# Layer 0 of a two-layer graph attention kernel: a pair's two aggregations in one set of matmuls, the tiles' chains staggered anew, and another order of loads and block sums at the begin

## Chip, core and metric

The kernel runs on one core of a Trainium2 chip. The metric is the device time of one execution in microseconds. One launch computes both layers, in float32 throughout.

## What is computed

The input `x` has 128 graphs of 64 nodes with 768 features, `adj` is a boolean adjacency per graph. Layer 0 is an additive graph attention with a gate, layer 1 a dot-product attention with six heads. Each is followed by a residual and a layer normalization. Cut to what matters here, layer 0 is:

```python
h = einsum('bnd,ade->bane', x, W)                 # 12 heads of 64
th = tanh(h)
attn = th @ w_src + swapaxes(th @ w_dst, 2, 3)    # rows + columns
attn = where(attn >= 0, attn, 0.2 * attn)
attn = softmax(where(~adj, -999.0, attn), axis=-1)
f = elu(einsum('banm,bame->bane', attn, h) + b)   # the aggregation
gate = sigmoid(x @ H_w.T + H_b)
x = layernorm(x + gate * f + (1 - gate) * x)
```

Layer 1 forms queries, keys and values with `Wq`, `Wk`, `Wv`, takes a masked softmax per head, and projects with `Wf`.

## The kernel before

Two graphs make a tile of 128 rows (nodes) by 768 features, so there are 64 tiles. Two tiles make a pair (`p` from 0 to 31, its tiles `i` = 0 and 1). Layer 0 (`phase_a`) goes over the pairs, and layer 1 (`phase_b`) over groups of two pairs.

**Dense products.** A product of a pair's two tiles with a 768 by 768 matrix is done with seven block products in place of eight, over sums of token blocks (`sums`, on POOL, L263 to L266) and sums of weight blocks (`weight_sums`, L178). Each of the seven is a *dense step* (`dense`): three matmuls of 128 by 128 by 384, two records each in the trace (L214), and an eviction. The evictions of i = 0, 2 and 3 are copies on ACT into `snap` (L439); those of i = 1, 4 and 5 are additions on DVE (L462, for V L481); that of i = 6 is a copy on ACT (L460, for V L479). The accumulators X (i = 0, 2, 4, 6), Z (i = 1) and Y (i = 3, 5) live in four PSUM banks (`psX`). Since i = 2 adds into the bank that i = 0 filled, its matmuls wait until the snap of i = 0 is taken; likewise i = 4 for the snap of i = 2, i = 5 for that of i = 3, and i = 6 for the addition of i = 4. Layer 0 does three products per pair: W gives h, G the gate's input, and V (a few pairs later, from the finished x1) layer 1's values.

**A tile's chain** (`Tile0`). From h: `tanh` (ACT, L499); products with `w_dst` and `w_src` (POOL, L503 and L511); their sums (DVE, L506 and L515) and a transpose (L508); the destination row goes out to DRAM and comes back over all partitions (`dst_out`, `dst_in`, L521 and L529, on SP's queue); `exchange` swaps halves of h by DMA (`hx`, L539); `add` (twelve ACT instructions, L553); `mask` and `top` (DVE, L560 and L564); `exp` (twelve ACT instructions, L569); `scale` (DVE reciprocal L577, POOL L579); `probs` (six transposes on TensorE, L590, and two copies on ACT, L595); `aggregate` (24 matmuls of 64 by 64 by 64, L608); `elu` (DVE L629, ACT L636); `mix1` and `mix2` (DVE, L641, L642, L650, L651); `norm1` (DVE L305 to L316 and three small ones on POOL, L317 to L322); `norm2` (ACT, L326); `spill` (DMA). `gate_in` (POOL, L618) and `gate` (ACT, L622) prepare the gate. x is loaded twice: as rows (`load`, into `xb`), and in blocks (`xp`), which DVE transposes (L418) into T.

**The order** is written out by hand: `at(step, f)` puts f into a list for its step, and `run` emits the lists in order of steps. Within a step the functions come in the order in which they were put there, pair by pair; the older pair's come first. Each engine works through its instructions in exactly this order. Pair p begins at step `O[p]`; below, o is that step:

```python
O = [14 * p if p < 3 else 21 * p - 21 for p in range(NP)]
...
for i, s in ((1, o), (0, o + (4 if p == NP - 1 else 5))):
    ...
    at(s + 24, t.probs)
    at(s + 25, t.aggregate)
    at(s + 26, t.elu)
```

In the steady state (21 steps a pair) W has steps 0 to 6 of a pair's slot, G 7 to 13, and V of the pair three before it 14 to 20; the chain of the slot's pair runs on into the next slot. Tile 1's chain starts with s = o, tile 0's with s = o + 5. So tile 1 is aggregated at step 25 (step 4 of the next slot) and tile 0 at step 30 (step 9). A few buffers are shared: one `th`, one `tmp`, one `z`, one `pt` (also the result of `elu`'s exponential), two `xp`, and four PSUM banks `pa`, of which an aggregation takes two until its `elu` has read them.

**The begin.** The first pair's x, the adjacency and W's four blocks are loaded in this order on SP's queue. The first pair's T comes from TensorE transposes (L433). DVE forms four weight block sums for each of three c before the first sum-dependent step, for W and later for H (`w1`), whose rows TensorE transposes (`hw_blocks`, L390).

Of the kernel before, what the change touches and what calls it, by code (L numbers as in the profile page):

```python
# [9 lines left out]
F32 = mybir.dt.float32  # L10
# [5 lines left out]
P = 128  # L16
# [45 lines left out]
def kernel(  # L62
# [31 lines left out]
    nc = tc.nc  # L94
    NB, S, D = x.shape
# [7 lines left out]
    NP = NT // 2  # L103
    assert S == 64 and DH == P and E == 64 and HALF == 384 and A == 12

    x_t = x.rearrange("(t g) n d -> t (g n) d", g=2)
# [7 lines left out]
    xb = const.tile([P, 7, D], F32, name="xb")  # L114
# [29 lines left out]
    def weight_tile(tag):  # L144
        return wts.tile([P, 7, CH, HALF], F32, name=f"w{tag}", tag=f"w{tag}")
# [28 lines left out]
    def weight_sums(part, eng, ks=range(4)):  # L174

        for k in ks:
            to, a, b = ((3, 6, 4), (4, 4, 0), (2, 6, 4), (5, 1, 2))[k]
            eng.tensor_tensor(part(to), part(a), part(b), ALU.subtract)  # L178
# [11 lines left out]
    def act_blocks(Ta, Tb, Ss):  # L190

        return [
            lambda c: Ta(c),
            lambda c: Ta(CH + c),
            lambda c: Ss(1, c),
            lambda c: Ss(2, c),
            lambda c: Ss(0, c),
            lambda c: Tb(CH + c),
            lambda c: Ss(3, c),
        ]  # L200
# [128 lines left out]
    def phase_a(ctx):  # L329
        k6 = ctx.enter_context(tc.tile_pool(name="k6", bufs=2))  # L330
        k3 = ctx.enter_context(tc.tile_pool(name="k3", bufs=1))
# [4 lines left out]
        st = [dict() for _ in range(NP)]  # L336
# [12 lines left out]
        def load_adj(p):  # L349
            t = small.tile([P, 2, S], U8, name="adj")  # L350
            nc.sync.dma_start(t, adj_p[p])
            st[p]["adj"] = t

        def load(p):
            st[p]["x"] = []
            for i in range(2):
                t = xb[:, (0, 1, 5, 6)[(2 * p + i) % 4]]
                nc.sync.dma_start(t, x_t[2 * p + i])
                st[p]["x"].append(t)

        load(0)
        load_adj(0)

        w0 = weight_tile(0)
        w0_v = w0.rearrange("p s c o -> p s (c o)").rearrange(
# [3 lines left out]
        for kh, oh in ((0, 0), (1, 0), (0, 1), (1, 1)):  # L369
            nc.sync.dma_start(  # L370
                w0_v[:, SLOT[kh, oh]],
                W_v[kh][:, oh * 6 : (oh + 1) * 6],
            )
        w1 = weight_tile(1)
        hrows = {}

# [65 lines left out]
        def sums(d):  # L442
            Ss = k6.tile([P, 4, CH, P], F32, name="S")
            token_sums(Ss, *d["T"])
            d["S"] = Ss

        def product(d, rhs, sink):
            Ta, Tb = d["T"]
            Ss = d["S"]
            blocks = act_blocks(lambda c: Ta[:, c, :], lambda c: Tb[:, c, :], lambda k, c: Ss[:, k, c, :])  # L450
            return Product(
                lambda i, c: blocks[i](c), rhs, [P, HALF], snap, sink
            )
# [36 lines left out]
        class Tile0:  # L490
            def __init__(self, p, i):
                self.p, self.i, self.d = p, i, st[p]
                self.sd = sds[i]
                self.last = p == NP - 1

            def tanh(self):
                self.h = self.d["h"][self.i]
# [84 lines left out]

            def probs(self):

                self.pt = k3.tile([P, D], F32, name="pt").rearrange("p (j n) -> p j n", n=P)
                for q in range(2):
                    ps = psa.tile([P, CH, P], F32, name="pa")
                    for jj in range(CH):
                        j = q * CH + jj
                        nc.tensor.transpose(  # L590
                            ps[:, jj, :],
                            self.s[:, 2 * j : 2 * j + 2, :].rearrange("p h m -> p (h m)"),
                            ident,
                        )
                    nc.scalar.copy(self.pt[:, q * CH : (q + 1) * CH, :], ps)  # L595
# [76 lines left out]
        def at(step, *fs):  # L672
            events.setdefault(max(step, 0), []).extend(fs)
# [6 lines left out]
            d[key].evict(i)  # L680

        for c in range(CH):
            at(0, lambda c=c: weight_sums(lambda s: w0_v[:, s, :, c, :], nc.vector))
            for k in range(4):
                at(
                    13 + 4 * c + k,
                    lambda c=c, k=k: weight_sums(lambda s: w2[:, s, c], nc.gpsimd, [k]),
                )
# [11 lines left out]
        for p in range(NP):  # L700
            d, o = st[p], O[p]
            d["p"] = p
            if p:
                at(max(o - 20, 1), lambda p=p: load_adj(p))
                at(o + 10, lambda p=p: load(p))

            def xb_in(d, i):
                d.setdefault("xp", []).append(blocks(x_t[2 * d["p"] + i]))

            def xT(d, i):  # L710
                d.setdefault("T", []).append(turn(d["xp"][i]))

            if p:
                at(max(o - 20, 1), lambda d=d: xb_in(d, 0))
                at(max(o - 16, 1), lambda d=d: xb_in(d, 1))
                at(o - 6, lambda d=d: xT(d, 0))
                at(o - 5, lambda d=d: xT(d, 1))
                at(o - 4, lambda d=d: sums(d))
            else:
                at(0, lambda d=d: d.update(T=[transposed(t) for t in d["x"]]))  # L720
                at(0, lambda d=d: sums(d))
            at(o, lambda d=d: start_h(d))
            at(o + 7, lambda d=d: start_g(d))
            for i in range(7):
                at(o + i, lambda d=d, i=i: dense(d, "W", i))
                at(o + 7 + i, lambda d=d, i=i: dense(d, "G", i))
            for i, s in ((1, o), (0, o + (4 if p == NP - 1 else 5))):
                t = Tile0(p, i)
                at(s + 6 + (i == 0), t.tanh, t.cap)
                at(s + 7, t.dst_mul)  # L730
                at(s + 8, t.src_mul)
                at(s + 9, t.dst_sum, t.dst_out)
                at(s + 10, t.src_sum)
                at(s + 13, t.dst_in)
                at(s + 16, t.exchange)

                at(s + (15 if i else 17), lambda t=t: t.add(0))
                at(s + (16 if i else 17), lambda t=t: t.add(1))
                at(o + (14 if i else 16), t.gate_in)
                at(o + (17 if i else 18), t.gate)  # L740
                n = s - (i == 1)
                at(n + 18, t.mask, t.top)
                at(n + 19, lambda t=t: t.exp(0))
                at(n + 20, lambda t=t: t.exp(1))
                (at_front if i else at)(s + 21, lambda t=t: t.scale(0), lambda t=t: t.scale(1))
                at(s + 24, t.probs)
                at(s + 25, t.aggregate)
                at(s + 26, t.elu)
                at(s + 27, t.mix1)
                at(s + 28, t.mix2)  # L750
                at(s + 29, t.norm1)

                n = s + (0 if p == NP - 1 else 1)
                at(n + 30, t.norm2)
                at(n + 31, t.spill)

            def x1_in(d, i):
                d["xp", i] = blocks(x1_d[2 * d["p"] + i])

            def x1T(d, i, t):  # L760
                d["x1T", i] = t
                nc.sync.dma_start(xT_d[d["p"]][:, i], t)

            def x1_sums(d):
                d["T"] = [d["x1T", i] for i in range(2)]
                sums(d)

            if p < NP - 3:
                v = O[p + 3] + 14
                times = ((1, v - 19, v - 13), (0, v - 16, v - 10))  # L770
            elif p < NP - 1:

                v = O[-1] + (21 if p == NP - 3 else 28)
                times = ((1, v - 16, v - 7), (0, v - 15, v - 6)) if p == NP - 3 else (
                    (1, v - 13, v - 6), (0, v - 10, v - 5)
                )
            if p < NP - 1:
                for i, t0, t1 in times:
                    at(t0, lambda d=d, i=i: x1_in(d, i))
                    at(t1, lambda d=d, i=i: x1T(d, i, turn(d["xp", i])))  # L780
                at(times[1][2] + 1, lambda d=d: x1_sums(d))
            else:
                v = o + 45
                for i in range(2):
                    at(o + 43 - i, lambda d=d, i=i: x1T(d, i, transposed(d["x"][i])))
                at(o + 44, lambda d=d: x1_sums(d))
            at(v, lambda d=d: start_v(d))
            for i in range(7):
                at(v + i, lambda d=d, i=i: dense(d, "V", i))

        for c in range(CH):
            at(4 + c, lambda c=c: weight_sums(lambda s: w1[:, s, c], nc.vector))


        early_sums = {"S": {}}
# [1 line left out]
        o = O[-1]  # L797
# [477 lines left out]
```

## Time and profile before

| | |
|---|---|
| median of three runs | 2848.83 us (2848.54 to 2848.85) |
| profiled execution, its own time | 2848.75 us |
| its span, first to last instruction | 2847.0 us |
| mean granted TensorE clock | 0.997 |
| layer 0 (to the first L904 matmul) | about 1466 us |
| layer 1 | about 1381 us |
| TensorE idle, from the span and its busy time | 40.4 us |

The profiled execution stands for the runs: it differs from their median by 0.1 us. The page gives each engine's busy share, the span in 40 slices, and the chain of work that ended last. A row of a timeline is: start in us from the span's start, duration, engine, line, operation, output<-inputs, shapes, count, and in brackets the engine's idle time just before and what ended it. A row of the chain of waits is: start, duration, and the work on the chain. PE is TensorE's matmuls, DVE VectorE, ACT ScalarE, POOL GpSimd, and SP the queue that issues all DMAs.

### The profile page before, as it was taken

How to read it: one execution, taken by the hardware profiler on the slowest of the kernel's cores; microseconds unless marked ns; L12 is line 12 of the kernel's file. 1: busy time of each engine (PE TensorE's matmuls, PEld its weight loads, DVE VectorE, ACT ScalarE, POOL GpSimd, SP SyncE). 2: the span in 40 equal slices, each digit the busy share in tenths (PEclk: the TensorE clock that was granted, in tenths of full speed). 3: DMA queues.
4: the chain of work that ended last, by engine and by line, in shares of the span. 5: the costliest groups of instructions: out<-in, count | busy, mean ns of one | idle time of the engine just before them, and what ended most of it. 6: DMA issues, size and time to landing. Idle time of an engine off the chain costs nothing.

```text
span 2847.0 us, 50750 instructions
## 1 busy us (share of the span) xinstructions
PE 2806.6 (99%) x18108; PEld 2062.2 (72%) x18108; DVE 1853.4 (65%) x3724; ACT 1198.5 (42%) x3737; POOL 1546.6 (54%) x1653
## 2 busy tenths in 40 slices
PE   8899999999999999999999999999999999999998
PEld 5555565655655665556568888888888888888887
DVE  4887777877877777777764555555555555555556
ACT  4666656566565665656622211222211222211223
POOL 4755556555566555565536555446554456454455
PEclk9999999999999999999999999999999999999999
DMA  6434445345454454444551211212211212211222
GB/s 170 121 113 139 142 132 146 114 138 147 127 146 126 132 149 123 143 133 133 181 180 35 90 67 63 85 57 90 90 65 60 90 57 90 89 62 63 90 84 73
DMA packets 358684, 308.40 MB, mean 108 GB/s; under 512 B 226592, under 2 KB 304160, under 8 KB 358432
## 3 DMA queue, kind: packets, MB, share of 16 engines
q1 hardware_dynamic: 358432, 305.16, 34.7%
q8 instruction: 144, 2.36, 0.3%
q14 instruction: 108, 0.88, 0.1%
HBM read 191.41 MB, written 101.06 MB: 103 GB/s over the span
## 4 chain that ended last, share of the span: by engine, by line
PE 87%; DVE 5%; POOL 3%; DMA 2%; ACT 2%; issue 1%; SPq 1%; DVEq 0%; ACTq 0%; POOLq 0%
PE X L904 43%; PE X L214 37%; PE pb L1051 2%; PE pb L969 2%; PE pa L608 1%; PE pa L590 1%; DMA s<-dst_d 1%; PE pb L1027 1%; ACT s L553 1%; DVE z L650 1%; ACT s L569 1%; DVE z L641 1%; DVE s L560 0%; DVE w L178 0%; POOL w L178 0%
## 5 line engine op out<-in xcount | busy, mean ns | idle before, releaser
L214 PE MATMUL X<-w,S 128*128 128x384 f32 x2304 | 795.0, 490 | 9.8 <-DVE w L178 3.3
L214 PEld LDWEIGHTS X<-w,S 128*128 128x128 f32 x2304 | 429.9, 190 | 297.6 <-DVE w L178 5.2
L904 PE MATMUL X<-S,w 128*128 128x256 f32 x2752 | 635.4, 379 | 0.0
L214 PE MATMUL X<-w,T 128*128 128x384 f32 x1728 | 600.7, 490 | 7.6 <-ACT snap L439 6.1
L904 PEld LDWEIGHTS X<-S,w 128*128 128x128 f32 x2752 | 518.1, 190 | 68.0
L214 PEld LDWEIGHTS X<-w,T 128*128 128x128 f32 x1728 | 325.9, 191 | 235.7 <-ACT snap L439 18.5
L947 DVE TENSOR_TENSOR xs<-xs,X 128x256 f32<-128x256 f32 x512 | 210.0, 419 | 175.0 <-PE X L904 166.5
L904 PE MATMUL X<-w,Sc 128*128 128x256 f32 x1280 | 294.4, 381 | 0.3 <-DVE xs L947 0.3
L569 ACT ACTIVATE s<-s,nmx 128x64 f32<-128x64 f32 x768 | 256.2, 335 | 76.5 <-DVE nmx L564 76.5
L930 DVE TENSOR_TENSOR k<-k,X 128x256 f32<-128x256 f32 x320 | 132.8, 418 | 231.9 <-PE X L904 160.2
L904 PEld LDWEIGHTS X<-w,Sc 128*128 128x128 f32 x1280 | 241.6, 190 | 34.3 <-DVE xs L947 1.1
L930 DVE TENSOR_TENSOR q<-q,X 128x256 f32<-128x256 f32 x320 | 133.1, 419 | 193.6 <-PE X L904 153.8
L904 PE MATMUL X<-xb,w 128*128 128x256 f32 x1024 | 258.0, 382 | 0.4 <-ACT q L925 0.4
L326 ACT ACTIVATE xs<-xs,shift,rstd 128x768 f32<-128x768 f32 x62 | 63.5, 1024 | 436.6 <-POOL shift L322 425.6
L439 ACT COPY snap<-X 128x384 f32<-128x384 f32 x288 | 135.5, 470 | 229.0 <-PE X L214 226.2
L925 ACT ACTIVATE k<-X,bk_c 128x256 f32<-128x256 f32 x192 | 91.0, 474 | 316.1 <-PE X L904 316.1
L503 POOL TENSOR_TENSOR tmp<-th,wd_bc 128x768 f32<-128x768 f32 x64 | 148.7, 2324 | 129.5 <-ACT th L499 129.5
L904 PEld LDWEIGHTS X<-xb,w 128*128 128x128 f32 x1024 | 192.0, 190 | 27.9 <-ACT q L925 0.8
L553 ACT ACTIVATE s<-s,src 128x64 f32<-128x64 f32 x768 | 193.1, 335 | 32.6 <-DMA s<-dst_d 32.5
L925 ACT ACTIVATE q<-X,bq_c 128x256 f32<-128x256 f32 x192 | 91.0, 474 | 273.7 <-PE X L904 273.7
L886 POOL TENSOR_TENSOR w<-cT 128x256 f32<-128x256 f32 x32 | 23.3, 728 | 333.6 <-PE X L904 332.4
L317 POOL TENSOR_TENSOR rstd<-rstd,neg_half 128x1 f32<-128x1 f32 x126 | 69.3, 550 | 232.3 <-DVE rstd L316 230.6
(123 smaller groups left out, 4280.5 us busy)
## 6 DMA issues: line engine op xcount, KB each, us to landing
xb<-in_x_dram SPq DMA_DIRECT2D x64, 384.0 KB
s<-dst_d SPq DMA_DIRECT2D x128, 192.0 KB
x_d<-xb SPq DMA_DIRECT2D x64, 384.0 KB
xT_d<-T SPq DMA_DIRECT2D x64, 384.0 KB
v_d<-v SPq DMA_DIRECT2D x128, 192.0 KB
xb<-xT_d SPq DMA_DIRECT2D x32, 768.0 KB
xb<-v_d SPq DMA_DIRECT2D x256, 96.0 KB
xs<-x_d SPq DMA_DIRECT2D x64, 384.0 KB
```

The costliest lines, as they stand in the source:

```text
L214: nc.tensor.matmul(o, self.lhsT(i, c), rhs, start=first and c == 0, stop=last and c == CH - 1, skip_group_check=True,)
L317: nc.gpsimd.tensor_tensor(rstd, rstd, neg_half, ALU.pow)
L326: nc.scalar.activation(r, r, AF.Identity, bias=shift, scale=rstd)
L439: nc.scalar.copy(t, ps)
L503: nc.gpsimd.tensor_tensor(self.tmp, self.th, wd_bc, ALU.mult)
L553: nc.scalar.activation(self.s[:, a], self.s[:, a], AF.Prelu, bias=self.src[:, a : a + 1], alpha=LEAKY_ALPHA,)
L569: nc.scalar.activation(self.s[:, a], self.s[:, a], AF.Exp, bias=self.nmx[:, a : a + 1], accum_out=self.sm[:, a : a + 1],)
L904: nc.tensor.matmul(ps, self.lhsT(r, slot, c), self.rhs(r, slot, c), start=start and c == 0, stop=stop and c == 1, skip_group_check=True,)
L925: nc.scalar.activation(o[:, b], ps, AF.Identity, bias=bias[:, hd : hd + 1], scale=1.0 if positive else -1.0)
L930: nc.vector.tensor_tensor(o[:, b], o[:, b], ps, ALU.add if positive else ALU.subtract)
L947: nc.vector.tensor_tensor(o, o, ps, ALU.add if positive else ALU.subtract)
L969: nc.tensor.matmul(pc[own, q, i, j, :], qT[:, b, q, own], kT[:, b, q, own], start=True, stop=True,)
```

## The change

For the pairs 0 to 29 (`both`), the aggregations of both tiles are emitted one after the other at step 28, tile 1 first. Tile 0's chain starts with s = o + 3 in place of o + 5, and its second half of adds has a step of its own (21). What follows the aggregation gets its own steps: tile 1's elu, mix1, mix2, norm1, norm2 at 29, 30, 32, 34, 36 (before 26, 27, 28, 29, 31), tile 0's at 35, 36, 37, 39, 41 (before 31, 32, 33, 34, 36); pairs 0 to 2 have slightly earlier ones. The gate's tanh goes from steps 17 and 18 to 25 and 26. Tile 1's transposed weights are put into the buffer of `z`, since both tiles' are now alive at once. From pair 4 on, the transposes of x (DVE) go from steps -6 and -5 to -4 and -3 and the token sums from -4 to -3; x's rows are loaded at step 16 in place of 10. The first pair's second x1 tile is read back three steps later. The last pair's tile 1 has its transposes and its aggregation one step earlier.

At the begin, x's second tile is loaded between W's second and third blocks, the adjacency after W, and the first pair's transposes are split around W's first dense step. W's sums come as three for each c, and the fourth ones (for i = 5) a step later; H's likewise.

```diff
@@ phase_a, the begin
         def load(p):
-            st[p]["x"] = []
             for i in range(2):
-                t = xb[:, (0, 1, 5, 6)[(2 * p + i) % 4]]
-                nc.sync.dma_start(t, x_t[2 * p + i])
-                st[p]["x"].append(t)
-
-        load(0)
-        load_adj(0)
+                load_tile(p, i)
+
+        def load_tile(p, i):
+            t = xb[:, (0, 1, 5, 6)[(2 * p + i) % 4]]
+            nc.sync.dma_start(t, x_t[2 * p + i])
+            st[p].setdefault("x", []).append(t)
+
+        load_tile(0, 0)
...
                 w0_v[:, SLOT[kh, oh]],
                 W_v[kh][:, oh * 6 : (oh + 1) * 6],
             )
+
+            if (kh, oh) == (1, 0):
+                load_tile(0, 1)
+        load_adj(0)
@@ Tile0.__init__
                 self.last = p == NP - 1
+                self.both = p < NP - 2
@@ Tile0.probs
-                self.pt = k3.tile([P, D], F32, name="pt").rearrange("p (j n) -> p j n", n=P)
+                self.pt = k3.tile([P, D], F32, name="z" if self.i and self.both else "pt").rearrange("p (j n) -> p j n", n=P)
@@ the order
         for c in range(CH):
-            at(0, lambda c=c: weight_sums(lambda s: w0_v[:, s, :, c, :], nc.vector))
+            at(0, lambda c=c: weight_sums(lambda s: w0_v[:, s, :, c, :], nc.vector, range(3)))
+            at(1, lambda c=c: weight_sums(lambda s: w0_v[:, s, :, c, :], nc.vector, [3]))
...
-                at(o + 10, lambda p=p: load(p))
+                at(o + 16, lambda p=p: load(p))
...
-                at(o - 6, lambda d=d: xT(d, 0))
-                at(o - 5, lambda d=d: xT(d, 1))
-                at(o - 4, lambda d=d: sums(d))
+                at(o - (4 if p > 3 else 6), lambda d=d: xT(d, 0))
+                at(o - (3 if p > 3 else 5), lambda d=d: xT(d, 1))
+                at(o - (3 if p > 3 else 4), lambda d=d: sums(d))
             else:
-                at(0, lambda d=d: d.update(T=[transposed(t) for t in d["x"]]))
-                at(0, lambda d=d: sums(d))
+                at(0, lambda d=d: d.update(T=[transposed(d["x"][0])]))
+                at(1, lambda d=d: d["T"].append(transposed(d["x"][1])))
+                at(1, lambda d=d: sums(d))
...
-            for i, s in ((1, o), (0, o + (4 if p == NP - 1 else 5))):
+            both = p < NP - 2
+            tiles = []
+            for i, s in ((1, o), (0, o + (3 if both else 4 if p == NP - 1 else 5))):
                 t = Tile0(p, i)
+                tiles.append(t)
...
-                at(s + (16 if i else 17), lambda t=t: t.add(1))
+                at(s + (16 if i else 18 if both else 17), lambda t=t: t.add(1))
                 at(o + (14 if i else 16), t.gate_in)
-                at(o + (17 if i else 18), t.gate)
+                if both:
+                    at(o + (25 if i else 26), t.gate)
+                else:
+                    at(o + (17 if i else 18), t.gate)
...
-                at(s + 24, t.probs)
-                at(s + 25, t.aggregate)
+                if both:
+                    at(s + 24, t.probs)
+                    if i == 0:
+                        at(o + 28, tiles[0].aggregate, tiles[1].aggregate)
+                    if i:
+                        e = (29, 30, 32, 34, 36) if p > 2 else (29, 30, 31, 33, 35)
+                    else:
+                        e = (35, 36, 37, 39, 41) if p > 2 else (32, 33, 34, 36, 38)
+                    for k, f in zip(e, (t.elu, t.mix1, t.mix2, t.norm1, t.norm2)):
+                        at(o + k, f)
+                    at(o + e[-1] + 1, t.spill)
+                    continue
+
+                n = s - (p == NP - 1 and i == 1)
+                at(n + 24, t.probs)
+                at(n + 25, t.aggregate)
...
-                times = ((1, v - 19, v - 13), (0, v - 16, v - 10))
+                times = ((1, v - 19, v - 13), (0, v - (16 if p else 13), v - (10 if p else 9)))
...
         for c in range(CH):
-            at(4 + c, lambda c=c: weight_sums(lambda s: w1[:, s, c], nc.vector))
+            at(4 + c // 2, lambda c=c: weight_sums(lambda s: w1[:, s, c], nc.vector, range(3)))
+            at(6, lambda c=c: weight_sums(lambda s: w1[:, s, c], nc.vector, [3]))
```

More of the change, by code (lines that the diff above doesn't have):

```diff
@@ L447, in product @@
         def product(d, rhs, sink):
-            Ta, Tb = d["T"]
-            Ss = d["S"]
-            blocks = act_blocks(lambda c: Ta[:, c, :], lambda c: Tb[:, c, :], lambda k, c: Ss[:, k, c, :])
+            blocks = act_blocks(
+                lambda c: d["T"][0][:, c, :], lambda c: d["T"][1][:, c, :], lambda k, c: d["S"][:, k, c, :]
+            )
             return Product(
```

## The prediction

> **What bounds the kernel now.** I read the page first, then the chain of waits for one pair, then the timelines of DVE, ACT and POOL at the same place.
>
> ```profile
> PE 2806.6 (99%) x18108; PEld 2062.2 (72%) x18108; DVE 1853.4 (65%) x3724; ACT 1198.5 (42%) x3737; POOL 1546.6 (54%) x1653
> PE   8899999999999999999999999999999999999998
> ACT  4666656566565665656622211222211222211223
> PE X L904 43%; PE X L214 37%; PE pb L1051 2%; PE pb L969 2%; PE pa L608 1%; PE pa L590 1%; DMA s<-dst_d 1%; PE pb L1027 1%; ACT s L553 1%; DVE z L650 1%; ACT s L569 1%; DVE z L641 1%; DVE s L560 0%; DVE w L178 0%; POOL w L178 0%
> ```
>
> TensorE is the bound: the engine sums of stretches put it at 1168.1 busy of 1170 us between 190 and 1360 us, the steady part of layer 0. ACT's low mean hides that in layer 0 it works at six tenths. The chain of waits from 764 to 812 us shows one pair:
>
> ```profile
> 768.28 0.86 PE pa L608 x48
> 769.14 29.22 PE X L214 x90
> 798.37 0.66 PE pa L590 x6
> 799.02 1.94 PE X L214 x6
> 800.96 0.86 PE pa L608 x48
> 801.82 8.07 PE X L214 x24
> ```
>
> A dense step (six records of L214) takes 1.94 us; L590 (a tile's transposes) costs 0.66; L608 is one tile's aggregation, 48 records. A pair takes 44.06 us from its first W step to the next pair's. No wait shows, but that doesn't say how near the others are. On DVE, the same pair:
>
> ```profile
> 782.98 0.56 DVE L481 TENSOR_TENSOR v<-X,snap 128x384 f32<-128x384 f32 x1 [0.55 <-PE X L214]
> 784.30 0.95 DVE L515 TENSOR_REDUCE src<-th 128x12 f32<-128x768 f32 x1 [0.76 <-POOL th L511]
> 785.17 2.49 DVE L418 STREAM_TRANSPOSE T<-xp 128x384 f32<-128x384 f32 x4
> 787.57 1.08 DVE L560 TENSOR_TENSOR s<-s,cap 128x768 f32<-128x768 f32 x1
> 788.68 0.95 DVE L564 TENSOR_REDUCE nmx<-s 128x12 f32<-128x768 f32 x1
> 789.55 0.55 DVE L481 TENSOR_TENSOR v<-X,snap 128x384 f32<-128x384 f32 x1
> ```
>
> The first L481 belongs to V's second step (i=1), the last to i=4. The matmuls of i=6, which add into the bank that i=4's eviction reads, start at 790.46: 0.36 us of slack. The mask (L560, L564) releases tile 1's exponentials on ACT:
>
> ```profile
> 789.73 0.35 ACT L569 ACTIVATE s<-s,nmx 128x64 f32<-128x64 f32 x1 [1.66 <-DVE nmx L564]
> ...
> 794.46 0.46 ACT L479 COPY v<-X 128x384 f32<-128x384 f32 x1
> 794.82 0.48 ACT L439 COPY snap<-X 128x384 f32<-128x384 f32 x1
> 796.25 2.97 ACT L553 ACTIVATE s<-s,src 128x64 f32<-128x64 f32 x12 [0.96 <-DMA s<-dst_d]
> ```
>
> The snap of the next pair's W step i=0 (794.82) stands ahead of tile 0's twelve adds (L553) and ends 1.0 us before W's i=2 starts (796.27). Tile 0's exponentials run on to 805.7, with the snap of i=3 between their halves, ending 0.05 us before i=5 starts (803.81). So TensorE bounds a pair, and one DVE-ACT chain has no slack left.
>
> **What the Trainium skill says.** "TensorEngine Tiling (Array Packing)", section Key Properties: changing the tiling mode drains TensorE. The trace agrees: a 64x64 set starts 0.416 us after the last dense matmul's start where dense ones follow at 0.323, and the dense matmuls after it lose another 0.25. "PSUM — Partial Sum Buffer", section Engine vs sequencer instructions: the queues of ScalarE, VectorE and GpSimd are strict FIFO; no DVE or ACT timeline here contradicts it. "SBUF — State Buffer", section SBUF: two separate sides: VectorE operations with two SBUF inputs and GpSimd operations take a shared port pair in turn, each for a whole instruction. The trace agrees: L641 at 762.57 lasted 1.58 us and ended 0.82 us after POOL's scaling (L579) had ended at 763.33; alone it takes 0.95.
>
> **Part 1, one set for two aggregations: a gain.** Of one set, by starts: 0.093 to get in, 0.716 inside, 0.148 to the next dense matmul, 0.104 more at the first: 1.06 us, twice a pair. Layer 0 shows no set of 96 records, but layer 1's contexts (L1051) are such sets: 95 gaps of 15.1 ns, 1.436 us. One merged set: 0.093+1.436+0.148+0.104 = 1.78. Saved 2.12-1.78 = **0.34 us a pair**, 30 pairs, 10.2 us. Bound above by 0.39, if the 87 ns gap that stands once in a set of before also falls away, and below by 0.29, if it comes a second time.
>
> **Part 2, the chains staggered anew: the loss.** In the changed instruction order, around V of each steady pair (slots of pairs 4 to 29), DVE has: V i=1's eviction, then all four mixing operations of the previous pair's tile 0 (L641, L642, L650, L651), this pair's mask and maximum (L560, L564), two transposes (L418), only then V i=4's eviction. ACT has: twelve exponentials of tile 1, V i=6's copy, the normalization L326, all twelve adds of tile 0, then W i=0's snap, twelve exponentials of tile 0, then W i=2's snap. With zero at the first eviction's start, which stays tied to TensorE, and start-to-start spacings from the trace of before:
>
> - DVE: eviction 0.47, L641 0.98, L642 0.99, L650 0.99, L651 0.88, L560 1.00, L564 0.87, transposes 1.20, so i=4's eviction starts at 7.38 and ends at 7.93. TensorE wants i=6 at 7.48 (790.46-782.98): **0.5 us late**.
> - L564 starts at 5.31, ends at 6.26; exponentials from 6.36 (0.10 later, as at 789.63/789.73), 12 at 0.333 to 10.36; copy 0.36, normalization 0.93, adds 2.88 to 14.53, snap 0.46 to 14.99. TensorE wants W i=2 at 13.29 (796.27-782.98): late by 1.75 in all.
> - Adds are done at 14.63, L560 and L564 to 16.58, exponentials 16.68 to 20.68, snap to 21.14. W i=4 follows i=2 by two steps and a tile's transposes, 4.53 us, so it is wanted at 15.04+4.53 = 19.57: **1.62 more**.
>
> That is 3.37 us a pair, less 0.34: **+3.0**. In the old order the last deadline was i=5, with the two aggregation and transpose groups ahead of it.
>
> POOL adds to this. The gate inputs (L618, 1.82 us each) now follow tile 1's norm: G i=5's eviction is three steps before zero (-5.81); sums, statistics and rstd put POOL's L317 at -2.67, the gate inputs at -1.63 and +0.16, the second ending at 1.98. L641 is ready at 0.47, waits, and ends at 2.80 instead of 1.42: **1.38 more**, total 4.75, net +4.4. If POOL is a little earlier it is less, down to nothing. I take **+4.0**: mostly with the conflict. The ends are 3.0 and 4.7. For 26 slots: +104, ends +78 and +122. Slot 30 has the V part alone: +1 (0.5 to 2).
>
> Edits that go with it: the gate tanh moves eight steps later on ACT, out of tile 1's exponentials (0.83 us less ahead of them; counted above by its absence). Tile 1's transposed weights in z cost no instruction; z is free until step 29 because mixing of tile 0 before ended at step 16. Holding four pa banks to step 35 blocks nothing: the next transposes are at step 45. The load of x (two DMAs on SP) goes from step 10 to 16, behind a spill and ahead of tile 1's exchange and tile 0's destination row (L529). SP issues the loads in 0.83 us, and what follows them is needed at step 20 or later, four steps (7.7 us) on. Taken at nothing; if that cover were gone, the adds would wait for L529's landing, as they did 0.96 us at 796.25.
>
> **Part 3, the begin.** W's blocks bound the start by bandwidth: the first DVE sum starts at 15.48 either way, as the same bytes come first. Three sums per c instead of four put the last one that i=2 needs ninth, not eleventh: 2 x 0.57 = 1.1 us of the 1.33 us wait at 21.78. H's sums for i=2 no longer stand behind the cap (1.83 us at 34.83): the 1.54 us wait at 39.86 goes. Together -2.6; bounds -3.3 (the three waits on L178) and +1 if x's second tile, now behind two blocks, is late for its transposes. Next late: the token sums on POOL, 4 us.
>
> **Part 4, pairs 0 to 3 and the last.** Pairs 14 steps apart had 13.2 us of TensorE idle between 62 and 190 us. The same merging there is worth 4 x 0.34 = -1.4. Whether the new order loses there isn't read off one row: between -5 and +12; I take +3. Last pair's tile 1 moves one step earlier on TensorE, where it waited 2.5 us at 1425: between -2 and +2, taken as 0.
>
> **Sum.** 104+1-2.6-1.4+3 = +104. The profiled execution took 2848.75 us (span 2847.0), the median of the runs is 2848.83: the same. Forecast **2953 us**.
>
> **Rivals.**
> - *TensorE stays the only bound* (faster): 10.2+2.6 saved, 2836 us. The place is W i=4 of the next pair; it decides if the chain from V i=1's eviction to W i=2's snap is no longer than 17.8 us, not 21.1. For it: the old chain to i=3's snap is 20.8 us and hidden. Against: its deadline was one step and an aggregation later. Chance 0.10.
> - *No port conflict* (slower, less): 26 x 3.0 in place of 104, 2927. For it: POOL's place rests on a chain of nine spacings. Chance 0.27.
> - *A second port conflict*: tile 0's destination product (L503) takes the port ahead of L651 at step 11, by a margin of 0.1 us, and G i=6 waits 1.1 more: 2953+29 = 2982. Chance 0.10.
> - *The stalls come out near the saving*: within 0.2%, 0.04.
> - *The change doesn't do what it says*: excluded, the new order has the 48 small matmuls of a pair in a row.
>
> The forecast itself has 0.49. The range, **2905 to 2985**, takes in the low end (26 x 3.0, early pairs -5, begin -3.3: 2917) with some room for shorter stalls, and the second conflict; outside are the faster case and no change. 0.2% (5.7 us) is about what a measurement here can tell from no change. Faster 0.10, same 0.04, slower 0.86.
>
> **What would show it.** Right: TensorE waits for DVE's v (V i=4) and for ACT's snap twice per pair, L641 of tile 0 above 2 us, a pair taking 47 to 49 us, one L608-like group of 96 records. Wrong: steady pairs of 43.7 us without waits on snap.

## The result, and the profile after

| | before | after |
|---|---|---|
| median of the runs (4 each) | 2848.68 us | 3234.17 us (3225.29 to 3235.89) |
| span of the profiled execution | 2847.0 us | 3233.1 us |
| mean granted TensorE clock | 0.997 | 0.952 |
| a steady pair, first W matmul to the next pair's (mean over the 21 slots of pairs 8 to 28) | 44.2 us | 57.7 us |
| first W matmul of the last pair | 1367.0 us | 1740.8 us |

The ratio is 1.135, 95% interval 1.134 to 1.136: slower by 385 us, where 104 were forecast. Layer 1 takes what it took (1381 us). The page of after, lines as they were shown of before (busy times, three rows of the 40 slices, and the chain's shares by line):

```profile
PE 2887.0 (89%) x18108; PEld 2103.4 (65%) x18108; DVE 1777.1 (55%) x3724; ACT 1199.6 (37%) x3737; POOL 1512.8 (47%) x1653
PE   8887878878788787887878899999999999999998
ACT  3655444444454444454445422221212222222223
PEclk9998998989989899998999999999999999999999
PE X L937 38%; PE X L214 25%; DMA s<-dst_d 6%; ACT s L559 4%; DVE T L423 2%; DMA xp<-x_d 2%; PE pb L1084 2%; DVE z L648 2%; PE pa L615 2%; PE pa L597 1%; PE pb L1002 1%; DVE s L566 1%; POOL S L263 1%; DVE z L657 1%; POOL S L264 1%
```

TensorE lost its full slices through layer 0, no other engine became full instead, and a transfer (s<-dst_d) leads the rest of the chain. PE's busy time even rose by 80 us, with the same number of matmuls: in the row of the granted clock (PEclk) many slices have dropped to eight tenths. The chain of waits of one pair says which transfer and why (start, duration, work; the next pair's W starts at 994.73):

```profile
983.48 0.56 DVE v L486
984.03 2.10 DVE z L648
...
990.87 1.26 DVE T L423 x2
992.13 0.03 DVE v L486
992.16 2.43 DMA xp<-x_d
...
998.41 0.19 SPq L535
998.60 0.04 issue
998.64 5.25 DMA s<-dst_d
1003.93 0.04 issue
1003.97 2.97 ACT s L559 x12
1006.95 0.37 ACT snap L444
1007.32 0.14 issue
1007.45 3.67 PE X L214 x6
```

It goes from DVE's transposes of x (xT, L423, which the change moves from step 15 to 17) to SP's reload of x1 for V (x1_in, xp<-x_d), which goes out as the first tile's transposes end, at 992.13 (the 0.03 us of L486 between them belong to V i=4's eviction, which had just begun), then to tile 0's destination row (dst_in, L535), its adds (L559), the snap of W i=0 behind them, and W i=2. SP's own timeline at the place:

```profile
984.06 0.35 SPq L487 DMA_DIRECT2D v_d<-v  x1
992.16 2.57 SPq L416 DMA_DIRECT2D xp<-x_d  x4
994.83 0.55 SPq L675 DMA_DIRECT2D x_d<-xb  x1
995.43 1.00 SPq L360 DMA_DIRECT2D xb<-in_x_dram  x2
996.53 0.66 SPq L545 DMA_DIRECT2D hx<-xb  x1
997.23 0.64 SPq L546 DMA_DIRECT2D hx<-xb  x1
997.97 1.26 SPq L535 DMA_DIRECT2D s<-dst_d  x2
```

SP stands from 984.41 to 992.16. There are two xp buffers, and x1_in, at step 16 of the slot, needs the one that xT reads. xT now comes at 17, and on DVE behind the mixing and the mask. The spill, the two loads of x, the exchange and dst_in wait behind x1_in in SP's order. Counted from the next pair's first W step, dst_in goes out at +3.25 us (before: -0.57), and the adds start at +9.87 (before: +3.79), in the mean of the 21 slots. The waits of PE in after (us in total, times, longest):

```profile
PE X L214 <- ACT snap L444: 272.0, 36, 9.9
PE X L214 <- DVE v L486: 42.0, 29, 2.7
```

After such a wait TensorE starts slowly. The engine sums of two stretches of another pair, from W i=2 on (the column after the five engines is the granted clock):

```profile
950.00:955.40 5.40, 5.21 (x12) 3.31 (x13) 3.44 (x6) 3.69 (x23) 0.83 (x1) 0.50 0.40 136
955.40:960.00 4.60, 4.60 (x16) 2.82 (x15) 1.71 (x4) 3.50 (x10) 3.71 (x5) 0.95 0.68 190
```

For 5.4 us the clock is at 0.50, and matmuls start every 640 ns where they start every 323 at full clock.

### The profile page after: what moved, and what is told of

Its sections match the earlier page's. It is cut to its first block, busy times and chain, and to the rows that moved or that the text cites. A ratio compares the mean times of both kernels' runs of the same rounds, so it can differ in the third digit from the quotient of the medians.

```text
span 3233.1 us, 50752 instructions
## 1 busy us (share of the span) xinstructions
PE 2887.0 (89%) x18108; PEld 2103.4 (65%) x18108; DVE 1777.1 (55%) x3724; ACT 1199.6 (37%) x3737; POOL 1512.8 (47%) x1653
## 4 chain that ended last, share of the span: by engine, by line
PE 70%; DVE 9%; DMA 9%; ACT 5%; POOL 3%; issue 2%; SPq 1%; DVEq 0%; POOLq 0%; ACTq 0%
PE X L937 38%; PE X L214 25%; DMA s<-dst_d 6%; ACT s L559 4%; DVE T L423 2%; DMA xp<-x_d 2%; PE pb L1084 2%; DVE z L648 2%; PE pa L615 2%; PE pa L597 1%; PE pb L1002 1%; DVE s L566 1%; POOL S L263 1%; DVE z L657 1%; POOL S L264 1%
## 5 line engine op out<-in xcount | busy, mean ns | idle before, releaser
L214 PE MATMUL X<-w,S 128*128 128x384 f32 x2304 | 858.8, 522 | 317.1 <-ACT snap L444 272.0
L214 PEld LDWEIGHTS X<-w,S 128*128 128x128 f32 x2304 | 454.9, 204 | 656.1 <-issue 365.6
L559 ACT ACTIVATE s<-s,src 128x64 f32<-128x64 f32 x768 | 193.8, 335 | 265.3 <-DMA s<-dst_d 261.7
L509 POOL TENSOR_TENSOR tmp<-th,wd_bc 128x768 f32<-128x768 f32 x64 | 136.2, 2128 | 308.9 <-ACT th L505 308.9
L585 POOL TENSOR_TENSOR s<-s,rs 128x384 f32<-128x384 f32 x128 | 105.2, 834 | 334.2 <-DVE rs L583 329.0
L566 DVE TENSOR_TENSOR s<-s,cap 128x768 f32<-128x768 f32 x64 | 64.1, 1001 | 336.9 <-ACT s L559 161.7
```

The lines of the kernel that those rows point to most:

```text
L214: nc.tensor.matmul(o, self.lhsT(i, c), rhs, start=first and c == 0, stop=last and c == CH - 1, skip_group_check=True,)
L509: nc.gpsimd.tensor_tensor(self.tmp, self.th, wd_bc, ALU.mult)
L559: nc.scalar.activation(self.s[:, a], self.s[:, a], AF.Prelu, bias=self.src[:, a : a + 1], alpha=LEAKY_ALPHA,)
L566: nc.vector.tensor_tensor(self.s, self.s, c, ALU.min)
L585: nc.gpsimd.tensor_tensor(t, t, rs[:, :, None].to_broadcast([P, A // 2, S]), ALU.mult)
```

## The experiments

The theory to be tested: **SP's queue**. The hold of x1_in, and the loads of x ahead of dst_in, make tile 0's row land late; the adds, the snap behind them and W i=2 follow, and the clock falls. What remains without it should be the forecast's chain on DVE and ACT. The rival is **bandwidth**: the loads of x take the rings when dst_in wants them, and the hold is beside the path. All numbers of single runs are against 2847 to 2853 us of the kernel before on the same chip. The time of a pair is the mean over the 21 slots of pairs 8 to 28, and so are the moments of dst_in and of the adds (both of tile 0), counted from the next pair's first W step.

**1. dst_in first.**

```diff
-                at(s + 13, t.dst_in)
+                (at_front if both and i == 0 else at)(s + 13, t.dst_in)
```

> The changed kernel with one edit: tile 0's load of its broadcast scores (dst_in, still step 16 of a slot) is put at the front of its step, ahead of the reload of x1 for V (x1_in) and of the two loads of x in SP's order. Queue theory (SP stands 7.8 us at x1_in for an xp buffer whose reader, the moved transpose xT, is now two steps later, and dst_in is queued behind it): the adds of tile 0 no longer wait 8.2 us, W i=0's snap behind them is in time, the pair falls from 57.8 us to the 48 us of the forecast's DVE-ACT chain, total 2960 to 3000 us. Bandwidth theory (the x loads, 786 KB, in front of dst_in on the DMA rings): the same 48 us, since dst_in is ahead of them too; the next two runs part the two. A third, that the scores are late because they are computed late: nothing moves, 3234 us.

Measured: 3027.4 us, 50.0 us a pair. SP still stands at x1_in until the same moment as in after (-2.57), but dst_in is out at -10.16 and the adds start at +1.61, without a wait in any of the 21 slots. More than half of the loss was in this landing.

**2. and 3. One of the two moves undone.** In run 2 (and 4) pair 2's and pair 3's loads come before the last spills of pairs 0 and 1 and overwrite their tile 0, so that their output is wrong there; no instruction is added or left out. The first diff is run 2's, the second run 3's.

```diff
-                at(o + 16, lambda p=p: load(p))
+                at(o + 10, lambda p=p: load(p))
```

> The changed kernel with the loads of x back at step 10 of the slot, where the kernel before has them. Queue theory: SP still stands at x1_in until xT has run; only the time in which the two loads share the rings with dst_in goes, about 4 us of 57.8: 53 to 54 us a pair, total 3110 to 3140 us. Bandwidth theory: dst_in lands soon after its issue, 48 us a pair, total about 2960 us.

```diff
-                at(o - (4 if p > 3 else 6), lambda d=d: xT(d, 0))
-                at(o - (3 if p > 3 else 5), lambda d=d: xT(d, 1))
-                at(o - (3 if p > 3 else 4), lambda d=d: sums(d))
+                at(o - 6, lambda d=d: xT(d, 0))
+                at(o - 5, lambda d=d: xT(d, 1))
+                at(o - 4, lambda d=d: sums(d))
```

> The changed kernel with xT and the block sums back at steps 15, 16 and 17 of the slot for all pairs (after's 17, 18, 18 for pairs from 4 on). Queue theory: the xp buffer is free when SP reaches x1_in, the 7.8 us stand goes, dst_in is behind the two loads of x alone: 48 to 51 us a pair, total 2960 to 3060 us. Bandwidth theory: the loads of x still stand ahead of dst_in, 54 us or more a pair, total over 3130 us.

Measured: 3137.5 us (54.6 a pair) and 3130.7 us (54.0). Neither theory alone: each move undone brings about 100 us. In run 2 dst_in goes out at +2.21, the adds start at +6.56; in run 3 at -2.45 and +4.43. There SP's stand at x1_in falls from 7.8 to 4.0 us (before: 1.9), and x1_in goes out at -8.25. From dst_in's issue to the adds it is 4.4 us without the loads ahead (before: 4.4), and 6.6 and 6.9 with them (after and run 3), besides their 1.0 us of issue. Run 3 also pays on DVE: with the transposes back ahead of V i=4's eviction, V loses 3.5 us a pair (after: 1.7).

**4. Both undone**, by the two diffs above.

> The changed kernel with both moves undone, the loads of x back at step 10 and xT and sums back at steps 15 to 17: what is left is the merged set and the new stagger of the chains. Forecast's chain (V i=4's eviction 0.5 us late, two late snaps 3.4 us, the port conflict at the first mix 1.4 us, less 0.34 for the merged set): 48 us a pair, total about 2953 us, with TensorE waiting for v and twice for snap. Rival, the chains are hidden once the loads are in time: 43.7 us a pair, total 2835 to 2850 us. Rival, another transfer is late: over 50 us a pair.

Measured: 3041.7 us, 50.9 a pair. The two gains add up (97 and 103, together 192), and what stays is more than the forecast's whole +104. It isn't another late transfer, the expected reason for over 50 us: the adds start at +1.92, with no wait in 20 of the 21 slots. V loses 3.9 us a pair here (after: 1.7), as in run 3.

**5. Only the hold taken away.** x1_in moves behind dst_in; DVE's order, the loads and dst_in keep their steps.

```diff
-                times = ((1, v - 19, v - 13), (0, v - (16 if p else 13), v - (10 if p else 9)))
+                times = ((1, v - (17 if p > 2 else 19), v - 13), (0, v - (16 if p else 13), v - (10 if p else 9)))
```

> The changed kernel with one transfer moved: the reload of x1 for V's first tile from step 16 to step 18 of the slot, behind tile 0's dst_in (16) and the transposes xT (17, 18) in program order. DVE's order stays that of the changed kernel. Queue theory: dst_in no longer stands behind the wait for the xp buffer, only behind the two loads of x: the wait of W i=2 for its snap falls from 9.3 us by the hold's 5 to 6 us, to about 4 us; pair 57.7 to about 52 us, total about 3085 us. Bandwidth theory alone: 57 us, total over 3200 us.

Measured: 3035.1 us, 50.0 a pair: 199 us less, nearly all that run 1 brought (207), though the loads of x stand ahead of dst_in. SP's timeline there (the next pair's W at 895.11):

```profile
885.34 1.01 SPq L360 DMA_DIRECT2D xb<-in_x_dram  x2
...
888.21 1.28 SPq L535 DMA_DIRECT2D s<-dst_d  x2
...
893.35 2.57 SPq L416 DMA_DIRECT2D xp<-x_d  x4
```

dst_in is out at -6.90 here (mean -7.15), before SP comes to x1_in. I had expected 4 us of wait to be left; I had taken the two shares for terms of a sum. It is a threshold instead: the adds start at +1.61 in this run as in run 1, when ACT is free, and only a landing after that costs anything. With 5.7 to 7.8 us from issue to adds behind the loads (the ends over all slots of after, run 3 and run 7) it isn't reached from -6.90.

**6. The same with the loads back at step 10**, which tells a threshold from a sum.

```diff
-                at(o + 16, lambda p=p: load(p))
+                at(o + (10 if p > 4 else 16), lambda p=p: load(p))
```

> The kernel with the reload of x1 at step 18 (3035 us), and in it the loads of x back at step 10 for pairs from 5 on. Threshold theory (tile 0's adds are late only by what dst_in's landing exceeds the moment at which ACT is free for them; in the 3035 us kernel dst_in is issued 8.5 us before that, and lands in 6 with the loads ahead of it): nothing more to gain, 3030 to 3040 us. Additive theory (the loads cost 97 us by themselves, as when they were moved in the changed kernel): about 2940 us.

Measured: 3034.3 us, with the adds again at +1.61. The threshold holds: the loads, worth 97 us in the changed kernel, are worth nothing here.

**7. The moves alone**, in the kernel before: its own lines for load, xT and sums set to after's steps.

```diff
-                at(o + 10, lambda p=p: load(p))
+                at(o + 16, lambda p=p: load(p))
...
-                at(o - 6, lambda d=d: xT(d, 0))
-                at(o - 5, lambda d=d: xT(d, 1))
-                at(o - 4, lambda d=d: sums(d))
+                at(o - (4 if p > 3 else 6), lambda d=d: xT(d, 0))
+                at(o - (3 if p > 3 else 5), lambda d=d: xT(d, 1))
+                at(o - (3 if p > 3 else 4), lambda d=d: sums(d))
```

> The kernel before with the two moves alone, the load of x from step 10 to 16 of the slot and xT and sums from 15, 16, 17 to 17, 18, 18 (pairs from 4 on), without the merged set and its stagger. Tile 0's dst_in is at step 18 here and its adds at 22. Queue theory: SP's stand before x1_in ends when xT has run at step 17, about when dst_in is due anyway, so that the hold costs little and the loads 2 to 4 us: 44.5 to 48 us a pair, 2860 to 2950 us. If the moves cost as much as they do in the changed kernel (7 us a pair): about 3030 us. If the load's old cover was free: 2849 us.

Measured: 3087.0 us, 52.9 a pair. My cheap case was wrong, the dear one (about 3030 us) still too low. The moves need no merged set to do harm. SP is held until the same moment as in after (x1_in at -2.51), dst_in goes out at +4.03 and the adds start at +10.48. Here another instruction pays. ACT's timeline in this kernel:

```profile
916.91 2.97 ACT L553 ACTIVATE s<-s,src 128x64 f32<-128x64 f32 x12 [7.34 <-DMA s<-dst_d]
919.79 0.46 ACT L439 COPY snap<-X 128x384 f32<-128x384 f32 x1
920.15 0.84 ACT L595 COPY pt<-pa 128x384 f32<-128x384 f32 x2
```

and PE's:

```profile
920.67 0.36 PE L608 MATMUL pa<-xb,pt 64*64 64x64 f32 x1 [5.15 <-ACT pt L595]
```

The adds hold up the copies of tile 1's transposed weights, and its aggregation waits 5.15 us.

**8. The two gate inputs on POOL later**, and ACT's tanh that reads them, on the kernel of run 5: the forecast's port conflict taken away.

```diff
-                at(o + (14 if i else 16), t.gate_in)
+                at(o + (25 if p > 3 and both else 14 if i else 16), t.gate_in)
-                    at(o + (25 if i else 26), t.gate)
+                    at(o + (30 if p > 3 else 25 if i else 26), t.gate)
```

> The kernel with the reload of x1 at step 18 (3035 us), and in it the two gate inputs on POOL at step 25 in place of 14 and 16, their tanh at 30 in place of 25 and 26, for pairs from 4 on. Forecast's port conflict (the gate inputs hold back tile 0's first mix, L648, 1.4 us, on the DVE-ACT chain): L648 takes 1 us or so in place of 2.2, V i=6 and the two late snaps come about 1.2 to 1.7 us earlier, 48.5 us a pair in place of 50, about 2995 us. Rival, the conflict is beside the path: 3035 us. Rival, the tanh or the gate inputs meet something else in their new place: over 3035 us.

Measured: 3014.9 us, 49.2 a pair: 20 us less, where 40 were expected. DVE's timeline:

```profile
877.06 0.95 DVE L648 SCALAR_TENSOR_TENSOR z<-pt,z 128x768 f32<-128x768 f32 x1
...
881.59 0.96 DVE L566 TENSOR_TENSOR s<-s,cap 128x768 f32<-128x768 f32 x1 [0.60 <-ACT s L559]
```

L648 takes 0.95 us in place of 2.16: the conflict was real, 1.2 us. But then the mask, L566, waits 0.60 us for tile 1's adds: half the gain went into the next wait.

**9. Pairs 0 to 3 as before**, on the kernel of run 5 (the first edit stands at both places of the condition).

```diff
-            both = p < NP - 2
+            both = 3 < p < NP - 2
...
-                at(o + 16, lambda p=p: load(p))
+                at(o + (16 if p > 4 else 10), lambda p=p: load(p))
```

> The kernel with the reload of x1 at step 18 (3035 us), and in it pairs 0 to 3 with two sets and the old stagger and loads, as in the kernel before; pairs from 4 on stay. If the new stagger of the early pairs, 14 steps apart, is what makes the first W step of pair 5 come 25 us later than before: 15 to 25 us less, 3010 to 3020 us. If it is the begin's order or the steady pairs' transfers running into slots 3 and 4: within 5 us of 3035.

Measured: 3021.5 us, 13.5 less. Pair 3's first W step comes at 113.4 us (before: 113.5) in place of 128.6. Pairs 3 to 5 still take 56.9, 55.0 and 52.9 us (before: 56.3, 47.0, 44.1).

**10. The begin alone**, in the kernel before: load order, split block sums, pair 0's transposes and first reload as in after. Its core:

```diff
-        load(0)
-        load_adj(0)
+        load_tile(0, 0)
...
+            if (kh, oh) == (1, 0):
+                load_tile(0, 1)
+        load_adj(0)
...
-            at(0, lambda c=c: weight_sums(lambda s: w0_v[:, s, :, c, :], nc.vector))
+            at(0, lambda c=c: weight_sums(lambda s: w0_v[:, s, :, c, :], nc.vector, range(3)))
+            at(1, lambda c=c: weight_sums(lambda s: w0_v[:, s, :, c, :], nc.vector, [3]))
...
-            at(4 + c, lambda c=c: weight_sums(lambda s: w1[:, s, c], nc.vector))
+            at(4 + c // 2, lambda c=c: weight_sums(lambda s: w1[:, s, c], nc.vector, range(3)))
+            at(6, lambda c=c: weight_sums(lambda s: w1[:, s, c], nc.vector, [3]))
```

> The kernel before with the begin's edits alone: x's second tile loaded behind two blocks of w0, the mask last, the block sums of w0 and w1 split, the transposes and the sums of pair 0 in two steps, pair 0's first reload three steps later. Forecast: 2.6 us less, about 2846 us, with W i=0 starting 1.5 us earlier and the wait for w1 at 39.9 us gone. Rival, that TensorE's clock comes up later in this order: G's first matmul at 36 us in place of 33.0, 2 to 3 us more, about 2851 us. Rival, other engines set the end of the begin: within 1 us of before.

Measured: 2849.35 against 2850.16 us (medians of 13 and 17 runs), ratio 0.9999, interval 0.9991 to 1.0007: the third case. W i=0 starts 1.8 us earlier (8.35), pair 0 takes 2.8 us longer (41.0), and at the end of layer 0's dense steps 0.5 us is lost.

**11. Another stagger, the merged set kept.** For the pairs from 4 on, dst_in goes to the front of its step, xT to 15 and 17 with the sums at 17, the gate's tanh to 30, and the reload of x1's tile 0 from step 19 to step 2 of the next slot, with the transposes of the reloads at 20 and at 5 of the next slot (in after 1 and 4 of the next). The rest of the edit (s is o for tile 1, o+3 for tile 0):

```diff
-                at(s + (15 if i else 17), lambda t=t: t.add(0))
-                at(s + (16 if i else 18 if both else 17), lambda t=t: t.add(1))
-                at(o + (14 if i else 16), t.gate_in)
+                at(s + (15 if i else 14 if both and p > 3 else 17), lambda t=t: t.add(0))
+                at(s + (16 if i or both and p > 3 else 18 if both else 17), lambda t=t: t.add(1))
+                at(o + ((15 if i else 25) if p > 3 and both else 14 if i else 16), t.gate_in)
...
-                        e = (29, 30, 32, 34, 36) if p > 2 else (29, 30, 31, 33, 35)
+                        e = (29, 29, 32, 32, 36) if p > 3 else (29, 30, 32, 34, 36) if p > 2 else (29, 30, 31, 33, 35)
-                        e = (35, 36, 37, 39, 41) if p > 2 else (32, 33, 34, 36, 38)
+                        e = (34, 35, 38, 41, 43) if p > 3 else (35, 36, 37, 39, 41) if p > 2 else (32, 33, 34, 36, 38)
```

> The changed kernel with another stagger for pairs from 4 on, the merged set kept: dst_in of tile 0 at the front of step 16; tile 0's adds at 17 and 19 (20 and 21 in the changed kernel), ahead of the snap of the next W i=0; its gate's add at 25 and both gates' tanh at 30; tile 1 elu and first mix at 29, second mix and norm at 32; tile 0 elu 34, mix 35 and 38, norms 41 and 43; xT at 15 and 17; the reloads of x1 at 16 and at 2 of the next slot. If what is left over the kernel before is only DVE's and ACT's order (queue theory with the forecast's chain): 43.8 to 46 us a pair, total 2870 to 2930 us; the merged set alone would make 43.7. If the merge itself forces a stall, because tile 0 must be ready 2 steps earlier: 48 us or more a pair, over 2980 us.

Measured: 2905.0 us, 45.4 a pair. Its waits of PE:

```profile
PE X L214 <- ACT snap L444: 29.9, 20, 5.7
PE X L214 <- DVE v L486: 27.7, 29, 2.8
```

Of the 13.4 us a pair that the change added, 12.2 come back with no operation taken out, merely by where the chains and the transfers stand. It doesn't beat the kernel before; what is left a pair is mostly the wait for V i=4's eviction (1.0 us), behind the transposes of x's second tile. No version run here is faster than it.

## Why the prediction was wrong, step by step

**The account of the 385 us.** Tile 0's late row, with the clock that falls after it: 199 (after less run 5; 26 slots at 7.6). DVE's and ACT's chain: 26 slots at 5.8 (50.0 less 44.2) = 151. Early pairs: 14 (run 9). The remaining 22 or so, in run 5's trace, are mostly in the slots of pairs 4 and 5 (13 above the 5.8 each) and in pair 30's slot and the dense steps after it (10); their causes stay open. The forecast had 104 for the chain, 3 for the early pairs and nothing for the row; none of its rivals was a late transfer.

**The step that failed: "Taken at nothing; if that cover were gone, the adds would wait for L529's landing".** The mechanism was named, but priced with the loads of x alone, counted from a free SP. Two things were left out. xT was followed on DVE, where it holds V i=4's eviction, and not to its buffer: the reload of x1, one step ahead on SP, waits for it. And the cover of 7.7 us was counted from step 16, while dst_in stood behind a hold already in the kernel before. Its waits of SP, not read then, show it; the second line is of after, where the wait is put down to L486, the eviction that starts just before the transposes end:

```profile
SPq L411 <- DVE T L418: 57.6, 30, 5.9
SPq L416 <- DVE v L486: 231.3, 28, 9.3
```

Thirty times a reload waited on SP for DVE's transposes, 1.9 us each, and dst_in's landing came 1.0 us after ACT was free (mean of the 21 slots). There was no cover to spend. In after it is 28 times and 8.3 us each, and the row costs 199 us where the forecast took nothing.

**The chain: right in its course.** Run 5 shows it without the late row. DVE's rows (zero of the forecast is the first):

```profile
883.88 0.56 DVE L486 TENSOR_TENSOR v<-X,snap 128x384 f32<-128x384 f32 x1 [1.09 <-ACT pt L643]
884.36 2.16 DVE L648 SCALAR_TENSOR_TENSOR z<-pt,z 128x768 f32<-128x768 f32 x1
...
892.45 0.50 DVE L486 TENSOR_TENSOR v<-X,snap 128x384 f32<-128x384 f32 x1
...
899.72 1.65 DVE L566 TENSOR_TENSOR s<-s,cap 128x768 f32<-128x768 f32 x1 [3.48 <-ACT s L559]
```

ACT's:

```profile
891.45 0.35 ACT L575 ACTIVATE s<-s,nmx 128x64 f32<-128x64 f32 x1 [2.29 <-DVE nmx L570]
...
899.60 0.46 ACT L444 COPY snap<-X 128x384 f32<-128x384 f32 x1
```

PE's:

```profile
900.20 2.17 PE L214 MATMUL X<-w,S 128*128 128x384 f32 x6 [1.06 <-ACT snap L444]
...
906.95 3.76 PE L214 MATMUL X<-w,S 128*128 128x384 f32 x6 [1.99 <-ACT snap L444]
```

| from zero, us | forecast with the conflict (1.38) | measured |
|---|---|---|
| V i=4's eviction starts | 8.76 | 8.57 |
| tile 1's exponentials start | 7.74 | 7.57 |
| snap of W i=0 ends, W i=2 can start | 16.37 | 16.18, 16.32 |
| snap of W i=2 ends, W i=4 can start | 22.52 | W i=4 at 23.07 |

**The chain's size: 4.0 forecast, 5.8 measured.** Two terms were missing. The last row is 0.5 us late because tile 0's mask (L566, 1.65 us in place of 0.95) starts together with the scaling on POOL, at 899.72: a third port conflict, it seems, that I hadn't looked for. In after, where this mask comes later, it takes 0.95 us; no run moved the scaling alone. And around the second stall the clock falls in 12 of the 21 pairs: there W i=4 and i=5 take 6.3 us together in place of 4.6; over all steady slots these two steps take 1.0 us more. The second conflict that the forecast had as a rival, with L651, didn't come: that instruction (L658 after) takes 0.96 us.

**The merged set: right.** In after its 95 gaps are 14.8 ns each (1.410 us), entered in 0.416 us and left in 0.148: 1.76 us by the forecast's sum, 1.78 forecast. That saves 0.37 us a pair, within the forecast's bounds.

**The begin: wrong, no effect.** Forecast -2.6 of its own, measured -0.3 with -2.6 as the end of the interval (run 10). Of the two waits that were to go, the one at 39.86 went; the one at 21.78 didn't (1.48 us at 20.87 in run 10). And the granted clock, full from 13.18 us on in before, is full there from 14.40, and at half again from 21.23 to 24.64: pair 0's slot takes what the earlier start had given. With the same begin in run 9 the clock is full from 12.86 on and the second pair starts at 47.85 us (before: 48.35, run 10: 49.31), so the begin's worth moves with the clock by more than a microsecond.

**Early pairs: mis-sized.** +3 taken (and -1.4 for the merging), 13.5 measured, just outside the end of 12. Run 9 undoes the stagger and the loads of these pairs together; which of them costs it stays open.

**What would have shown it right**: the wait for v, L648 over 2 us (2.18) and the groups of 96 records are there; the wait for snap comes once a pair in after (36 in all) and twice in run 5 (62); the pair of 47 to 49 us isn't, not even in run 5 (50.0).

## What to carry to other kernels

When a step that reads a rotating buffer is moved later, ask who refills that buffer and on which queue, then list what stands behind that refill; on SP's in-order queue one held DMA delays every transfer behind it, whatever it is for. Price a late transfer as a threshold, its issue time plus issue-to-use against the moment its user is free, and not as a sum of shares: the same 97 us of loads were worth nothing once the issue was early. In a stream of matmuls, count on a slow restart after each stall of 3 us or more, and on a possible one after a stall of 2 us.

## What the runs showed of the hardware

**A stall costs TensorE more than its length, and where it falls decides.** Over after and runs 1 to 5, from 190 us on in layer 0, stalls between two dense matmuls were sorted by length (time between the two starts, less the usual 0.323 us). All 82 of 3 us or more were followed at once by matmuls at 640 ns. Of 109 with 2 to 3 us, 75 were, at once or within the next fifteen matmuls; of 205 with 1 to 2 us, none. In the pair of after above the half clock lasted 5.4 us and cost some 2.6.

The granted clock in the traces says which of the stalls in the middle pay. In each of the 13 traces it changes only on a grid of 3.413 us (607 changes in all, each within 1 ns of its trace's grid). None of 10656 stretches of this grid at full clock with less than 1.7 us of idle TensorE was followed by the half clock; all 232 with more than 2.02 us were, and 78 of the 119 between. Back to full it went after all 286 stretches at half clock with less than 0.39 us idle, and after none with more than 0.6. So a stall of 2 to 3 us costs a restart when nearly all of it lies in one stretch, and costs none when a boundary divides it well. In runs 1 and 5 W i=4 waits some 2.1 us in a pair, and the half clock comes in 12 of the 21 pairs of each.

The Trainium skill, "TensorE: Matmul & The Clock Gate", section "HAM oscillation — how this bites in real kernels", gives the rule as no idle gaps over about 3.4 us. The traces agree for the long stalls; for stalls of 2 to 3 us they show the half clock below that bound.

**What stands ahead in a queue delays a landing.** From dst_in's issue to the adds that waited for it, mean of the 21 slots: 4.4 us in before and in run 2, without the two loads of x issued ahead; 6.6, 6.9 and 6.5 in after and runs 3 and 7, with them. After and run 2 differ in the place of the loads alone. The skill's "DMA: Bandwidth & Descriptors", section "Queues, rings and completion order", says that each DMA engine consumes its descriptors in ring order; that fits, but no run here varied the size of the loads alone.
